# LayerNorm, attention and a SiLU feed-forward gate on one core: narrow attention matmuls joined, transposes and normalizations moved, the start reordered

## The chip, the cores and the metric

The kernel runs on one core of a Trainium2 chip. The metric is the time of the device for one execution, in microseconds, lower is better. A run gives one such time; the time of a kernel is the median of its runs. Besides, one execution was recorded by the hardware profiler: its span runs from the first to the last instruction.

The core has five engines that run their own queues of instructions in order and wait for each other by semaphores: TensorE (PE; its weight loads are shown as PEld), VectorE (DVE), ScalarE (ACT), GpSimd (POOL), and SyncE (SP), which here only issues DMAs. Matmul results go to PSUM, in 8 banks; everything else lives in SBUF.

## The reference

```python
xn = layernorm(x)                                    # x: (4, 512, 512), over the last axis
q, k, v = (einsum('bpd,hde->bphe', xn, W) + b for W, b in ((W_Q, b_Q), (W_K, b_K), (W_V, b_V)))
scores = einsum('bqhe,bkhe->bhqk', q, k) / sqrt(128) # 16 heads of 128
attn = softmax(where(causal, scores, -1e5), axis=-1)
z = einsum('bkhe,bhqk->bqhe', v, attn)
s = einsum('bqhe,hed->bqd', z, W_O) + b_O
g = (xn @ gate_w.T) * gate_s                         # gate_w, up_w: (1408, 512), entries -1, 0, 1
u = (xn @ up_w.T) * up_s
f = ((silu(g) * u) @ down_w.T) * down_s
out = x + s * silu(f)
```

## The kernel before

Everything is float32. To keep that precision[...], each operand of a matmul is held as two tensors, a high part (rounded by a copy on ACT to fp32r) and a low part (the rest, by a subtraction, on DVE or POOL). A product is three matmuls, high x high, high x low and low x high: `mm3` (line 90) and `mm3_all` (line 95, all high x high first). The class `Split` carries the pair.

The program runs in two stages, each written in a fixed order by hand (`tc.manual_schedule()`): the order of the calls is the order in every engine's queue. The first stage is LayerNorm and attention, up to line 635. The second is the feed-forward part with the final product (`ffn`, line 640), in a branch chosen by a flag computed in the first stage (whether the ternary weights are exact in fp32r; here they are, so `ffn(True)` runs).

Attention works on 64 "heads": 8 groups `g` of two heads (HG = 2), in each group four batches `b`, in each batch the two heads `i`; `heads` (line 526) is that list and `n` the index in it. The 512 rows of a batch are four tiles of 128. `xnT[b]` is the normalized input, transposed.

One pass of the loop at line 534, for head `n`, issues:
- `softmax` (line 280): scores of this head, query tile by query tile in the order 3, 2, then 1 and 0 packed, each only against the keys it may see (512, 384, 256 and 128 columns); DVE adds the mask and takes the row extreme (L306); ACT computes exp with the row sum (L320), DVE the reciprocal of the sum (L323), POOL scales the row (L324).
- `turn_p` (line 327): the probabilities are transposed, by 32x32 blocks on DVE (L338) and by two DMAs through DRAM (L343, L349); they come back in `raw`, for the next pass of the loop.
- `split_p` (line 354): high and low part of the probabilities of the head before, `pt`, in two halves of 128x640: ACT casts (L365), DVE subtracts (L366). In the first four passes and the last one it stands right behind `softmax`, in the others behind `turn_p`. The very last head uses `transpose_p` on PE instead.
- `project` (line 250), a generator: q, then k of the next head, each twelve matmuls of 512 columns into one PSUM bank; ACT adds the bias and writes the high part (L260), DVE the low part (L263). The first head alone is done in two halves (`parts` = 2), in one PSUM tile.
- `attend` (line 384) for the head before: z is 4 query tiles wide; key tile j = 0, 3, 1, 2 contributes to the query tiles from j on, so its matmuls have 512, 128, 384 and 256 columns, in three passes. ACT and DVE then write z with its bias, high and low (L399, L400).
- `fill`: the projection of v, a row tile at a time (`project_v`, line 242, twelve matmuls of 256 columns), in passes with i = 0, two tiles ahead of `turn_p` and two at the end; in passes with i = 1 `project_out` (line 413), the output projection of the group and batch before, accumulated in DRAM over the groups.
- `split_pending` (line 160): casts and subtractions of weights that have arrived. `prepare` (line 166) issues their loads: on SP at the start, on ACT's queue in the loop (line 525). The staging pool `rawp` has 4 buffers.

In the passes n = 0, 2, 4 (`ln_next`) the LayerNorm of the next batch is finished: `ln_normalize` (line 218) on DVE behind q's projection, then, at the end of the pass, `ln_transpose` (line 227): four PE transposes of 128x128 a tile, an ACT cast, and the low part on DVE (`ln_low`). The statistics (`ln_stats`, `ln_sd`) are taken in the passes 0, 1 and 3. The square root and the exp need different tables on ACT; `table` loads one ahead of its use.

PSUM: pool `ps_st` has 3 banks, tag "st" (scores, transposes of even tiles, the warm-up); pool `ps_mm` has 5, tag "mm" (v, q, k, z, output projection, transposes of odd tiles). A tile takes the bank that was given out longest ago, and waits until its last reader is done. `pp`, the pool of the probabilities, has one buffer.

The start, lines 469 to 523, is written out: loads, twenty warm-up transposes (`warm_up`), statistics and normalization of batch 0 tile by tile, weight splits in between, and the first q, k and v.

## Time and profile before

| what | value |
|---|---|
| median of 3 runs (lowest, highest) | 1222.03 us (1222.0, 1223.22) |
| the profiled execution | 1223.04 us, its span 1221.2 us |
| PE clock granted over the span | 0.998 |
| instructions in the span | 18879 |
| POOL scaling the probabilities (L324), 256 of them | 148.8 us |
| DVE low part of the probabilities (L366), 126 | 133.0 us |
| ACT exp (L320), 256 | 140.9 us |
| DVE block transposes (L338), 378 | 113.3 us |

Busy time of the engines by stretch of the span, with the number of instructions in brackets; the columns are start and end, length, busy time of PE, PEld, DVE, ACT and POOL, PE's clock, the mean share of the DMA engines, GB/s:

```profile
0.00:22.00 22.00, 15.78 (x100) 13.87 (x101) 12.31 (x25) 11.65 (x23) 11.17 (x20) 1.00 0.55 176
22.00:50.00 28.00, 27.30 (x165) 23.64 (x164) 25.18 (x75) 16.31 (x35) 4.13 (x8) 1.00 0.48 157
50.00:100.00 50.00, 48.33 (x281) 41.93 (x281) 43.60 (x126) 30.31 (x67) 9.98 (x14) 1.00 0.45 136
...
400.00:600.00 200.00, 200.00 (x1129) 177.08 (x1129) 152.35 (x385) 90.19 (x212) 51.16 (x64) 1.00 0.66 201
```

The stretch from 0 to 22 us is the start, 22 to 100 holds the first passes with the LayerNorm of batches 1 to 3, the third kind is the steady middle. The attention stage ends near 974 us; behind it comes the feed-forward part. Matmuls are pipelined: a record's duration is longer than the distance to the next one's start, and that distance is what a matmul costs PE.

### The profile page before, as it was taken

What the parts mean: (1) busy time and instruction counts of PE and PEld (TensorE: products, weight loads), DVE (VectorE), ACT (ScalarE), POOL (GpSimd) and SP (SyncE); (2) the same over time, 40 slices, a digit from 0 to 9 for tenths busy, and PEclk for the clock granted to TensorE, in tenths of its full rate; (3) what the DMA queues carried; (4) which work ended last, traced back from release to release, by engine and by line L of the source; (5) the groups of instructions that cost most, each with busy time, mean ns of one, the idle gap of its engine ahead of it and who ended that gap; (6) DMA issues with size and microseconds to landing.
All of it is one profiled execution on the core that took longest, in us unless ns stands there. A gap on an engine that the chain in (4) does not pass through costs nothing.

```text
span 1221.2 us, 18879 instructions
## 1 busy us (share of the span) xinstructions
PE 1204.9 (99%) x6510; PEld 1049.7 (86%) x6510; DVE 827.3 (68%) x2044; ACT 526.0 (43%) x1169; POOL 303.2 (25%) x433
## 2 busy tenths in 40 slices
PE   7999999999999999999999999999999999999997
PEld 7878888888888888888888888888888888888886
DVE  6897777777777777777777676767677533434343
ACT  5654544444445445444544454445444342323231
POOL 4212321232124213321422141214121341212010
PEclk9999999999999999999999999999999999999999
DMA  4454456666675667666755565565544893737341
GB/s 161 134 177 146 142 171 199 197 193 192 190 207 173 198 201 210 180 199 201 222 182 173 178 190 170 174 191 174 173 156 156 270 317 94 207 87 212 82 147 38
DMA packets 117912, 215.55 MB, mean 177 GB/s; under 512 B 13232, under 2 KB 45744, under 8 KB 117808
## 3 DMA queue, kind: packets, MB, share of 16 engines
q1 hardware_dynamic: 74016, 134.51, 34.8%
q10 hardware_dynamic: 29376, 53.26, 14.5%
q0 software_dynamic: 14416, 26.48, 8.1%
q8 instruction: 53, 0.87, 0.3%
q14 instruction: 51, 0.42, 0.1%
HBM read 135.17 MB, written 79.04 MB: 175 GB/s over the span
## 4 chain that ended last, share of the span: by engine, by line
PE 95%; DVE 3%; ACT 1%; DMA 0%; issue 0%; SPq 0%; DVEq 0%; ACTq 0%
PE psv L103 14%; PE psq L103 14%; PE psk L103 14%; PE z L395 10%; PE pd L676 7%; PE pg L676 7%; PE pu L676 7%; PE pso L91 5%; PE pso L93 5%; PE pso L92 5%; PE sc L91 3%; PE sc L93 3%; PE sc L92 3%; DVE xn L224 1%; PE sc L297 1%; DVE xl L235 1%
## 5 line engine op out<-in xcount | busy, mean ns | idle before, releaser
L324 POOL TENSOR_SCALAR p<-p,rtot 128x512 f32<-128x512 f32 (+3 forms) x256 | 148.8, 603 | 673.7 <-DVE rtot L323 673.7
L320 ACT ACTIVATE p<-p,nmax 128x512 f32<-128x512 f32 (+3 forms) x256 | 140.9, 552 | 148.6 <-DVE nmax L306 148.6
L366 DVE TENSOR_TENSOR ptl<-ptr,pth 128x640 fp32r<-128x640 f32 x126 | 133.0, 1093 | 1.4 <-ACT pth L365 1.4
L338 DVE STREAM_TRANSPOSE sq<-p 128x256 f32<-128x256 f32 x378 | 113.3, 362 | 0.0
L306 DVE CUSTOM_DVE_ANT_0 p<-sc,mask 128x512 f32<-128x512 f32 (+2 forms) x192 | 96.5, 552 | 1.4 <-PE sc L93 1.4
L260 ACT ACTIVATE k<-psk,consts 128x512 fp32r<-128x512 f32 (+1 forms) x65 | 44.3, 681 | 108.7 <-PE psk L103 108.7
L260 ACT ACTIVATE q<-psq,consts 128x512 fp32r<-128x512 f32 (+1 forms) x65 | 44.3, 682 | 97.0 <-PE psq L103 71.7
L365 ACT CAST pth<-ptr 128x640 fp32r<-128x640 f32 x126 | 85.0, 724 | 0.8 <-DMA ptr<-turn 0.5
L421 DVE TENSOR_TENSOR a<-pso,a 128x512 f32<-128x512 f32 x108 | 72.1, 686 | 17.7 <-PE pso L93 17.7
L263 DVE SCALAR_TENSOR_TENSOR k<-psk,consts,k 128x512 fp32r<-128x512 f32 (+1 forms) x65 | 48.0, 738 | 52.9 <-ACT k L260 52.9
L702 DVE SCALAR_TENSOR_TENSOR hd<-pu,consts,sg 128x512 f32<-128x512 f32 x44 | 33.0, 751 | 66.7 <-PE pu L676 62.2
L323 DVE RECIPROCAL rtot<-tot 128x1 f32<-128x1 f32 x256 | 41.6, 163 | 42.7 <-ACT p L320 36.3
L91 PE MATMUL sc<-k,q 128*128 128x512 f32 (+2 forms) x192 | 65.9, 343 | 2.8 <-DVE xl L235 1.6
L93 PE MATMUL sc<-k,q 128*128 128x512 f32 (+2 forms) x192 | 64.7, 337 | 0.0
L92 PE MATMUL sc<-k,q 128*128 128x512 f32 (+2 forms) x192 | 64.7, 337 | 0.0
L263 DVE SCALAR_TENSOR_TENSOR q<-psq,consts,q 128x512 fp32r<-128x512 f32 (+1 forms) x65 | 47.6, 732 | 9.4 <-ACT q L260 9.4
L320 ACT ACTIVATION_READ_ACCUMULATOR p<-p,nmax 128x1 f32 x256 | 47.7, 186 | 0.0
L91 PEld LDWEIGHTS sc<-k,q 128*128 128x128 f32 x192 | 36.2, 188 | 9.2 <-DVE xl L235 3.5
L732 ACT ACTIVATE o<-o 128x512 f32<-128x512 f32 (+1 forms) x17 | 10.3, 607 | 68.8 <-DVE o L731 68.8
L92 PEld LDWEIGHTS sc<-k,q 128*128 128x128 f32 x192 | 36.2, 188 | 3.6
L93 PEld LDWEIGHTS sc<-k,q 128*128 128x128 f32 x192 | 36.1, 188 | 2.6
L700 ACT ACTIVATE sg<-pg,consts 128x512 f32<-128x512 f32 x44 | 30.3, 688 | 17.0 <-PE pg L676 17.0
(734 smaller groups left out, 3342.2 us busy)
## 6 DMA issues: line engine op xcount, KB each, us to landing
turn<-sq SPq DMA_DIRECT2D x63, 640.0 KB, 3.8
ptr<-turn SPq DMA_DIRECT2D x252, 160.0 KB, 3.4
acc<-a SPq DMA_DIRECT2D x124, 256.0 KB, 3.7
a<-acc ACTq DMA_DIRECT2D x108, 256.0 KB, 2.9
xt<-in_x SPq DMA_DIRECT2D x16, 256.0 KB, 4.2
wor<-in_w_o ACTq DMA_DIRECT2D x16, 256.0 KB, 4.9
fa<-acc SPq DMA_DIRECT2D x16, 256.0 KB, 5.7
fx<-in_x SPq DMA_DIRECT2D x16, 256.0 KB, 6.0
```

The source lines that it names most:

```text
L91: nc.tensor.matmul(ps, a.hi, b.lo, start=first, stop=False)
L92: nc.tensor.matmul(ps, a.hi, b.hi, start=False, stop=False)
L93: nc.tensor.matmul(ps, a.lo, b.hi, start=False, stop=last)
L103: nc.tensor.matmul(ps, l, r, start=n == 0, stop=n == len(todo) - 1)
L263: nc.vector.scalar_tensor_tensor(q.lo[:, at_], ps[:, at_], bias[:, h : h + 1], q.hi32[:, at_], ALU.add, ALU.subtract,)
L306: nc.vector.tensor_tensor_reduce(out=of[t], in0=where[t], in1=add, scale=-SCALE, scalar=BIG, op0=ALU.add, op1=ALU.min, accum_out=nmax[t],)
L320: nc.scalar.activation(of[t], of[t], AF.Exp, bias=nmax[t], scale=-1.0, accum_out=tot)
L324: nc.gpsimd.tensor_scalar(of[t], of[t], rtot, 1.0, ALU.mult, ALU.mult)
L338: nc.vector.transpose(dst.rearrange("p a s i -> p s a i"), src.rearrange("p (s a i) -> p s a i", s=n, i=Q),)
L366: nc.vector.tensor_tensor(dst(pt.lo), src, dst(pt.hi32), ALU.subtract)
L395: nc.tensor.matmul(o, v, p_, start=k == 0, stop=k == len(todo) - 1)
L676: nc.tensor.matmul(ps, l, r, start=first and k == 0, stop=last and k == len(pairs) - 1)
```

## The change

- `attend` gets an argument `joined`, true for the heads with index 9 to 60. There the passes run over the key tiles 0, 1, 2 only. Key tile 3 is computed apart in a PSUM tile `z2` of two parts: one matmul multiplies its high weights by the high and the low probabilities at once (256 columns), one adds low x high to the first part (128 columns). The probabilities' high and low parts lie in one tensor for that (`p_split`). ACT writes the first three query tiles from `z`; `z2` is copied to SBUF by ACT, its two parts and z's last tile are added on DVE, and the last query tile leaves from there.
- `split_p` gets `shared`: in the passes 9 to 61 the first half's subtraction goes to POOL.
- In the passes n = 2 and 4 the four normalizations of the next batch stand behind the four reciprocals of the softmax, one each, on DVE. In pass 0 they stay.
- In the passes 0, 2, 4 the sixteen transposes go one by one behind the matmuls of the last two v tiles, and the low parts with them (`side`), instead of all behind them.
- At the start the statistics of tiles 2 and 3 are taken together, ahead of the low parts of tiles 0 and 1; the exp table is loaded right after their square root; the low part of wv goes to DVE; wq and wk of the second head are split after the first head's q and k. `project` takes a PSUM tile for each part.
- Behind the last output projection stand eight more transposes of the identity, into a tile that nobody reads.

```diff
+LINGER = 8
...
         for n, (l, r) in enumerate(todo):
             nc.tensor.matmul(ps, l, r, start=n == 0, stop=n == len(todo) - 1)
+            if side:
+                side.pop(0)()
...
-        def split_w(dst, raw):
+        def split_w(dst, raw, on=nc.gpsimd):
             nc.scalar.copy(dst.hi, raw)
-            nc.gpsimd.tensor_tensor(dst.lo, raw, dst.hi32, ALU.subtract)
+            on.tensor_tensor(dst.lo, raw, dst.hi32, ALU.subtract)
...
-        def warm_up():
+        def warm_up(n=WARM):
...
-            for k in range(WARM):
+            for k in range(n):
...
         def ln_transpose(b, t):
+            for step in ln_transposes(b, t):
+                step()
+
+        def ln_transposes(b, t):
+
             xn = xn_of.pop((b, t))
             pool, tag = ((ps_st, "st"), (ps_mm, "mm"))[t % 2]
-            tr = pool.tile([P, ND, P], F32, name="tr", tag=tag)
-            for c in range(ND):
-                nc.tensor.transpose(tr[:, c, :], xn[:, ts(c, P)], ident)
             to = xnT[b][:, :, ts(t, P)]
-            nc.scalar.copy(to.hi, tr)
-            lo_of[b, t] = lambda: nc.vector.tensor_tensor(to.lo, tr, to.hi32, ALU.subtract)
+            tr = []
+
+            def step(c):
+                if c == 0:
+                    tr.append(pool.tile([P, ND, P], F32, name="tr", tag=tag))
+                nc.tensor.transpose(tr[0][:, c, :], xn[:, ts(c, P)], ident)
+                if c == ND - 1:
+                    nc.scalar.copy(to.hi, tr[0])
+                    lo_of[b, t] = lambda: nc.vector.tensor_tensor(
+                        to.lo, tr[0], to.hi32, ALU.subtract
+                    )
+
+            return [lambda c=c: step(c) for c in range(ND)]
...
-            ps = ps_mm.tile([P, S], F32, name="ps" + name, tag="mm")
...
             for k in range(parts):
                 at_ = ts(k, S // parts)
-                mm3_all(ps[:, at_], [(w[:, c, :], xnT[b][:, c, at_]) for c in range(ND)])
+                ps = ps_mm.tile([P, S // parts], F32, name="ps" + name, tag="mm")
+                mm3_all(ps, [(w[:, c, :], xnT[b][:, c, at_]) for c in range(ND)])
...
-        def softmax(qT, kT):
+        def softmax(qT, kT, between):
...
                     nc.vector.reciprocal(rtot, tot)
+                    if between:
+                        between.pop(0)()
                     nc.gpsimd.tensor_scalar(of[t], of[t], rtot, 1.0, ALU.mult, ALU.mult)
...
-        def split_p(raw):
-            pt = weight(pp, [P, NS, P], "pt", "pt")
+        def p_split():
+            both = pp.tile([P, 2, NS, P], F32R, name="pt", tag="pt")
+            pt = Split(both[:, 0], both[:, 1])
+            pt.both = both
+            return pt
+
+        def split_p(raw, shared):
+            pt = p_split()
...
-                nc.vector.tensor_tensor(dst(pt.lo), src, dst(pt.hi32), ALU.subtract)
+                on = nc.gpsimd if shared and k == 0 else nc.vector
+                on.tensor_tensor(dst(pt.lo), src, dst(pt.hi32), ALU.subtract)
...
-        def attend(h, pt, vs):
+        def attend(h, pt, vs, joined):
             z = ps_mm.tile([P, NT, P], F32, name="z", tag="mm")
+            last = NT - 1
+            e = ts(h % HG, E)
+            s_ = slot[last]
...
-                for j in (0, NT - 1, 1, 2):
-                    v = getattr(vs[j], part)[:, ts(h % HG, E)]
+                for j in range(last) if joined else (0, last, *range(1, last)):
+                    v = getattr(vs[j], part)[:, e]
...
+            if joined:
+                z2 = ps_mm.tile([P, 2, P], F32, name="z2", tag="mm")
+                nc.tensor.matmul(z2, vs[last].hi[:, e], pt.both[:, :, s_, :], start=True, stop=False)
+                nc.tensor.matmul(
+                    z2[:, 0], vs[last].lo[:, e], pt.hi[:, s_, :], start=False, stop=True
+                )
...
-            nc.scalar.activation(zT.hi, z, AF.Identity, bias=bias)
-            nc.vector.scalar_tensor_tensor(zT.lo, z, bias, zT.hi32, ALU.add, ALU.subtract)
+            def leave(at_, src):
+                nc.scalar.activation(zT.hi[:, at_], src, AF.Identity, bias=bias)
+                nc.vector.scalar_tensor_tensor(
+                    zT.lo[:, at_], src, bias, zT.hi32[:, at_], ALU.add, ALU.subtract
+                )
+
+            if not joined:
+                leave(slice(0, NT), z)
+                return zT
+            leave(slice(0, last), z[:, :last])
+            rest = small.tile([P, 2, P], F32, name="rest", bufs=1)
+            nc.scalar.copy(rest, z2)
+            nc.vector.tensor_tensor(rest[:, 0], rest[:, 0], rest[:, 1], ALU.add)
+            nc.vector.tensor_tensor(rest[:, 1], z[:, last], rest[:, 0], ALU.add)
+            leave(last, rest[:, 1])
             return zT
...
-            ln_stats(0, [2])
             split_pending(-4)
             ln_transpose(0, 0)
             ln_transpose(0, 1)
+            split_pending(-3)
+            ln_stats(0, [2, 3])
             ln_low(0, 0)
             ln_low(0, 1)
-            ln_sd(0, [2])
-            split_pending(-3)
-            ln_stats(0, [3])
-            split_pending(-2)
-            ln_sd(0, [3])
+            ln_sd(0, [2, 3])
+            table(AF.Exp)
             ln_normalize(0, 2)
             ln_normalize(0, 3)
+            split_pending(-2, nc.vector)
...
-            split_pending(-1)
-            table(AF.Exp)
             qT = next(q_of)
             kT = next(k_of)
+            split_pending(-1)
...
+                joined = B * HG < heads.index(before) < len(heads) - 3
...
+                norms = [lambda t=t: ln_normalize(b + 1, t) for t in range(NT)] if ln_next else []
+                of = softmax(qT, kT, norms if n > 0 else [])
...
-                    pt = split_p(raw)
+                    pt = split_p(raw, B * HG < n < len(heads) - 2)
...
-                    if ln_next:
-                        for t in range(NT):
-                            ln_normalize(b + 1, t)
+                    while norms:
+                        norms.pop(0)()
...
                 if ln_next:
+                    for t in range(NT):
+                        side.extend(ln_transposes(b + 1, t))
+                        side.append(lambda t=t: ln_low(b + 1, t))
                     fill(range(half, NT))
-                    for t in range(NT):
-                        ln_transpose(b + 1, t)
-                        ln_low(b + 1, t)
+                    while side:
+                        side.pop(0)()
...
+            warm_up(LINGER)
```

More of the change, by code (lines that the diff above doesn't have):

```diff
@@ L103, in mm3_all @@
             nc.tensor.matmul(ps, l, r, start=n == 0, stop=n == len(todo) - 1)
+            if side:
+                side.pop(0)()
+    side = []
     with ExitStack() as at:
@@ L158, with split_pending @@
         pending = []
-        def split_pending(n):
+        def split_pending(n, on=nc.gpsimd):
             for due, dst, raw in [p for p in pending if p[0] <= n]:
-                split_w(dst, raw)
+                split_w(dst, raw, on)
             pending[:] = [p for p in pending if p[0] > n]
@@ L257, in project @@
                 at_ = ts(k, S // parts)
-                mm3_all(ps[:, at_], [(w[:, c, :], xnT[b][:, c, at_]) for c in range(ND)])
+                ps = ps_mm.tile([P, S // parts], F32, name="ps" + name, tag="mm")
+                mm3_all(ps, [(w[:, c, :], xnT[b][:, c, at_]) for c in range(ND)])
                 yield
-                nc.scalar.activation(
-                    q.hi[:, at_], ps[:, at_], AF.Identity, bias=bias[:, h : h + 1]
-                )
+                nc.scalar.activation(q.hi[:, at_], ps, AF.Identity, bias=bias[:, h : h + 1])
                 nc.vector.scalar_tensor_tensor(
-                    q.lo[:, at_], ps[:, at_], bias[:, h : h + 1], q.hi32[:, at_],
-                    ALU.add, ALU.subtract,
+                    q.lo[:, at_], ps, bias[:, h : h + 1], q.hi32[:, at_], ALU.add, ALU.subtract
                 )
@@ L365, in split_p @@
                 nc.scalar.copy(dst(pt.hi), src)
-                nc.vector.tensor_tensor(dst(pt.lo), src, dst(pt.hi32), ALU.subtract)
+                on = nc.gpsimd if shared and k == 0 else nc.vector
+                on.tensor_tensor(dst(pt.lo), src, dst(pt.hi32), ALU.subtract)
             return pt
         def transpose_p(of):
-            pt = weight(pp, [P, NS, P], "pt", "pt")
+            pt = p_split()
             pairs = [(j, t) for j in range(NT) for t in range(j, NT)]
@@ L531, in attend_last @@
                 g, b, i = before
-                zs.setdefault((g, b), []).append(attend(g * HG + i, pt, v_of[g, b]))
+                joined = B * HG < heads.index(before) < len(heads) - 3
+                zs.setdefault((g, b), []).append(attend(g * HG + i, pt, v_of[g, b], joined))
             for n, (g, b, i) in enumerate(heads):
@@ L556 @@
                 if n == 1:
-                    pt = split_p(raw)
-                of = softmax(qT, kT)
+                    pt = split_p(raw, B * HG < n < len(heads) - 2)
+                norms = [lambda t=t: ln_normalize(b + 1, t) for t in range(NT)] if ln_next else []
+                of = softmax(qT, kT, norms if n > 0 else [])
                 if n > 1 and early:
-                    pt = split_p(raw)
+                    pt = split_p(raw, B * HG < n < len(heads) - 2)
                 look()
@@ L566 @@
                 if not early:
-                    pt = split_p(raw)
+                    pt = split_p(raw, B * HG < n < len(heads) - 2)
                 split_pending(n)
@@ L632 @@
             last = (NG - 1, B - 1)
-            zs[last].append(attend(H - 1, pt, v_of[last]))
+            zs[last].append(attend(H - 1, pt, v_of[last], False))
             for t in range(NT):
                 project_out(*last, t, zs[last])
+            warm_up(LINGER)
     def ffn(exact):
```

## The prediction

> **What bounds the kernel now.** I read the shares of part 1 of the page first, then the chain of part 4, then PE's waits over the whole run, then the timeline of one head in the middle, and last the chain and the timelines of the first 66 us.
>
> ```profile
> PE 1204.9 (99%) x6510; PEld 1049.7 (86%) x6510; DVE 827.3 (68%) x2044; ACT 526.0 (43%) x1169; POOL 303.2 (25%) x433
> ...
> PE 95%; DVE 3%; ACT 1%; DMA 0%; issue 0%; SPq 0%; DVEq 0%; ACTq 0%
> ```
>
> TensorE is the bound: 99% busy, 95% of the chain. Work on DVE, ACT or POOL counts only where PE waits for it. PE's waits (who, for whom, us, times, longest) are few, and all but the last lie before 67 us:
>
> ```profile
> PE sc L91 <- DVE xl L235: 1.6, 4, 0.6
> PE tr L232 <- DVE xn L224: 1.5, 3, 0.8
> PE warm L216 <- POOL ident masks.py:199: 1.4, 1, 1.4
> PE psq L103 <- DVE q L263: 1.4, 1, 1.4
> ...
> PE pg L676 <- PE pso L93: 0.9, 1, 0.9
> ```
>
> From 100 to 900 us PE has no wait at all; there only its own instruction stream can be shortened. One attention product (`attend`) in PE's timeline, columns start, duration, line, tiles, shape:
>
> ```profile
> 506.12 0.39 PE L395 MATMUL z<-pth,v_0h 128*128 128x512 f32 x1
> ...
> 506.35 0.22 PE L395 MATMUL z<-pth,v_3h 128*128 128x128 f32 x1
> ...
> 506.41 0.39 PE L395 MATMUL z<-pth,v_1h 128*128 128x384 f32 x1
> ...
> 506.64 0.28 PE L395 MATMUL z<-pth,v_2h 128*128 128x256 f32 x1
> ...
> 506.75 0.40 PE L395 MATMUL z<-pth,v_0l 128*128 128x512 f32 x1
> ...
> 508.04 0.64 PE L103 MATMUL psv<-wv4h,xh 128*128 128x256 f32 x4
> ```
>
> The distance of starts is the cost, not the duration. A pass of four takes 0.64 us, the twelve 1.92 (506.12 to 508.04). The 384-wide one takes 0.23 here; in the scores, where no narrow one stands before it, 0.175 (511.61, 511.78, 511.96). So a 128-wide matmul costs its 0.06 and about 0.06 more at its successor: 0.12, as much as a 256-wide one (0.117).
>
> **What the Trainium skill says.** "TensorE: Matmul & The Clock Gate", section Back-to-back issue gap: the spacing is set by weight load and matmul together. The trace agrees (128 columns cost as much as 256), but not with the page's 81 and 131 ns for N=128 and 512: here 120 and 230, which I use. "SBUF — State Buffer", section SBUF: two separate sides: DVE and POOL share a port pair as an exclusive lock, taken by a DVE op in a two-port mode, or with two SBUF inputs against a POOL op that reads SBUF. The trace agrees:
>
> ```profile
> 10.31 1.66 DVE L224 TENSOR_SCALAR xn<-xt,mv,rstd 128x512 f32<-128x512 f32 x1
> 10.39 2.70 POOL L145 TENSOR_TENSOR wv0l<-wvr,wv0h 128x512 fp32r<-128x512 f32 x2
> ```
>
> The same `xn` takes 0.55 where POOL is idle. "GPSIMD Engine Reference", section Engine selection: two-input elementwise work is about twice as slow on POOL; the trace has 1.29 us for a 128x512 subtraction on POOL and 0.69 on DVE.
>
> **Joined narrow matmuls (52 heads).** `joined` holds for head indices 9 to 60. Three 128-wide matmuls (key tile 3) leave the passes; one 256-wide (high values on high and low weights side by side) and one 128-wide come behind them, in another PSUM tile. Cost: 3 x (0.23 + 0.175 + 0.117) + 0.117 + 0.12 = 1.80. L297 and L298 of the scores are the same pair of shapes: 512.48, 512.60, 512.66, then 0.29 for a 512-wide one instead of 0.23, so the pair's price is measured. Gain 1.92 - 1.80 = 0.12 a head, 52 x 0.12 = **6.2 us**. Bounds: 0.13 a head (6.8) at best, 0 if new waits eat it.
>
> What it adds elsewhere, per head. ACT: one 0.69 becomes 384 wide (0.60 by the exp of that width), a copy of 256 (0.37, the v cast) and 128 wide (0.39): +0.67. DVE: 0.75 becomes about 0.60 + 2 x 0.285 + 0.29: +0.7; the shared `split_p` takes a 128x640 subtraction (0.77 to 0.81) off it: even. POOL gets that half: 1.29 x 640/512 = 1.6 us, 53 times. The work that hides all this is PE's 14.8 us per head. The new waits: ACT's last `leave` waits for two DVE adds; behind it stand the v casts (or the next exp, which waits for DVE anyway). After z ends at 508.0 the chain of four ACT and DVE steps is over by about 510.5; `pso` reads z first at 512.6. POOL's half starts when its normalizing ends (516.6) and ends near 518.2; the third pass reads it at 522.2. In the heads that also split weights, POOL's subtractions now block DVE's `ptl` (two take 3.56 at 532.92 instead of 1.52) and leave 0.5 us before the third pass; with one half gone from DVE this gets better. ACT's loads of raw weights wait for POOL in seven heads (q copied at 241.65 after 4.27 us of it, k's low part 0.77 before the scores); POOL idles 1.71 us just before, and the half fits there but for some 0.3. The PSUM ring of five now turns over eight tiles a head: `psv` of tile 3 takes the bank of the same head's `psq`, free at 505.5 (at 537.1 in the worst kind of head), needed at 509.3 (539.0). I take 0 for all of this.
>
> **The start (before 21.1).** Own PSUM tiles per half in `project` remove the 1.4 us wait of the second `psq` for the first half's DVE read. The low half of wv goes from POOL to DVE, so nothing locks `xn` of tiles 2 and 3 (1.66 and 1.30 become 0.55), and PE's 0.3 and 0.75 before their transposes go. Against this: the statistics of tile 3 (0.69 + 0.18) now stand on DVE ahead of both `xl`; the third pass of the first `psq` starts at 10.3 instead of 9.46. The Exp table (1.28 + 0.2) now sits on ACT ahead of the wv casts, which then end at 11.95, before `psv` wants them at 13.3; SP's queue is unchanged. Step by step: psk ends 12.4, transposes to 13.3, psv to 14.75, second psq at 14.75 instead of 16.87, less 0.1 for psk waiting on the first psq's bank. **Gain 2.0**, bounds 1.2 and 2.6.
>
> **Transposes between matmuls, and the norms (heads 0, 2, 4).** The chain in head 0 runs on DVE from 26.95 to 37.2: statistics, q, norms, k, v, xl. In head 0 the norms stay behind q's projection, so xn of tile 0 ends at 32.13, but its first transpose is now PE's second instruction of the fill, at 30.0: PE stops 2.1 us there. Then 39 instructions at 0.117 reach 36.7, and the scores run unhindered to 38.4. Before, tile 3's scores began at 34.80 and waited for xl; they ended at 37.90. **Cost 0.5.** In head 2 the norms go between the softmax reciprocals, where DVE idles 1.6 us in all. Each pair takes 0.65, and by the lock POOL's normalizing and DVE's norm exclude each other. Unlocked, `ptl` ends at 57.5, 0.45 after the third pass wants it, and the scores end at 64.8 instead of 66.64 (gain 1.8). Locked throughout it ends at 58.9, PE stops 1.9, and they end at 66.3 (gain 0.3). I take **0.7**, since rtot frees POOL about when the norm starts. In head 4 only 0.24 was lost (3.83 for transposes and scores against 3.59 of work): **0.2**.
>
> **LINGER.** Eight transposes behind the last `pso`: the first `pg` (974.62) waits for DVE's last `a_last` (973.72 + 0.69), so PE is idle from 973.5 and eight at 0.115 fill 0.9 of it. **Cost 0.1** for the last one's completion; bounds 0 and 0.9.
>
> **Sum.** 6.2 + 2.0 - 0.5 + 0.7 + 0.2 - 0.1 = 8.5 us. The profiled execution took 1223.04 (span 1221.2, 1.8 around it), which gives 1214.5; it lies 1.0 above the median of 1222.03, and against that I predict **1213.5**.
>
> **Rivals.**
> A. The head of the run gives nothing: ACT's table load and DVE's added work delay `psv`, and head 2 pays the lock in full. For: all steps there hang on 0.1 to 0.5 us. Against: the 1.4 of PSUM wait goes whatever else happens; 1.4 less the 0.8 of the later third pass leaves 0.6 of the 2.0, and head 2 turns from 0.7 to -0.4. 8.5 - 1.4 - 1.1 = 6.0: 1216.0.
> B. The middle is taken back by a new wait, for instance `psv` of tile 3 behind `psq`'s read where ACT waits for POOL. For: 0.77 us is the smallest distance found. Against: it exists in 7 heads of 52. Then only 2.3 remain: 1219.7.
> C. Slower. In-order ACT, blocked at the last `leave`, passes its delay on to the casts that free PSUM, and PE stops in every joined head. Place: psv of tile 3 and the first scores after it. It decides from 8.5/52 = 0.17 us of stop per head, which needs DVE's two adds some 2 us later than worked out (k's low part ends 2.7 to 3.05 before the scores in most heads). At 0.25 a head: 13 - 8.5 = 4.5: 1226.5. Against: DVE's load per head is unchanged.
> D. That joining changes nothing, because the pair costs three narrow ones: excluded by L297 and L298, save for the wider stride; counted in B.
>
> **How the numbers follow.** Forecast 0.73 (own range 1211.5 to 1216), A 0.12, B 0.10, C 0.05. The range 1210.5 to 1218.5 takes in A and the bounds of the terms (the start 0.6 better, head 2 1.1 better, a wait or two in the middle). 0.2%, 2.4 us, is what a measurement of this kernel can tell from no change; faster than 1219.6 are the forecast, A and half of B: 0.90; same 0.05, slower 0.05.
>
> **What will show it.** z's group with z2 at 1.80 from first start to the next matmul; no PE wait from 100 to 900; first scores near 19.1; a wait of about 2 us of the first transpose for xn in head 0; `ptl` against the third pass in head 2; `pg` within 0.2 of `a_last`. A PE wait for DVE or POOL that recurs in the joined heads would make the prediction wrong.

## The result: four microseconds faster, less than half of the forecast

| | before | changed |
|---|---|---|
| median of 8 runs each (lowest, highest) | 1222.39 us (1221.67, 1224.16) | 1218.81 us (1217.08, 1219.66) |
| ratio, 95% interval | | 0.9967 (0.9956 to 0.9977) |
| the profiled execution: time, span | 1223.04, 1221.2 us | 1218.36, 1217.0 us |

The kernel is 0.33% faster, 3.6 us by the medians. The forecast was 8.5 us and a range from 1210.5 to 1218.5; the median lies just outside it. The page after the change, parts 1 and 4 (busy us, share of the span, instructions; then the chain's shares):

```profile
PE 1199.1 (99%) x6466; PEld 1047.4 (86%) x6466; DVE 795.5 (65%) x2149; ACT 549.9 (45%) x1272; POOL 378.6 (31%) x484
...
PE 96%; DVE 2%; ACT 0%; DMA 0%; issue 0%; SPq 0%; DVEq 0%; ACTq 0%
```

TensorE is still the bound, with 44 matmuls fewer (52 saved, 8 idle ones added). All its waits, in the order of the forecast's list (who, for whom, us, times, longest):

```profile
PE z L423 <- DVE pt L391: 3.4, 1, 3.4
PE tr L247 <- DVE xn L230: 2.2, 2, 2.0
PE warm L222 <- POOL ident masks.py:199: 1.4, 1, 1.4
PE psq L104 <- DVE xl L250: 1.3, 1, 1.3
PE sc L92 <- DVE k L280: 1.1, 1, 1.1
PE psq L104 <- ACT xh L249: 0.7, 1, 0.7
```

All lie before 100 us. The first line is new and the largest: z's third pass in head 2 waits 3.4 us for the low part of the probabilities. The waits alone do not tell the price, though. ("z group" is the run of z matmuls of one `attend`.) To get the price, the first matmul of each of the 64 z groups, which the timeline gives to 0.01 us, was set against the same group of the kernel before. That difference is a running account; where it changes, something was won or lost:

| stretch, profiled executions | forecast, us | measured, us |
|---|---|---|
| start, to the first scores (21.09 to 19.03) | +2.0 | +2.06 |
| head 0, to the first z group | -0.5 | -0.58 |
| head 1, to the second z group | 0 | +0.23 |
| head 2, to the third (19.08 before, 21.86 after) | +0.7 | -2.78 |
| head 4, to the fifth | +0.2 | +0.35 |
| 52 joined heads (the account goes from -0.72 to +5.20) | +6.2 | +5.92 |
| LINGER, to the first `pg` | -0.1 | -0.08 |
| after the first `pg`, to the end of the span | 0 | -0.96 |
| sum | +8.5 | +4.16 |

The spans differ by 4.2, so the account is closed. Against the forecast's 8.5, 3.5 us are lost in head 2, 1.0 at the very end and 0.3 in the joined heads; some 0.4 more than forecast came in at the start and in heads 1 and 4, which leaves 4.3 missing. The start of one profile is good to 1 us only: in the ten other profiles below that have the changed start the first scores come at 18.03 to 18.92, here at 19.03. The joined heads read as forecast:

```profile
505.38 0.40 PE L423 MATMUL z<-pt,v_0h 128*128 128x512 f32 x1
...
505.91 0.28 PE L426 MATMUL z<-pt,v_3h 128*128 128x256 f32 x1
506.03 0.22 PE L427 MATMUL z<-pt,v_3l 128*128 128x128 f32 x1
506.09 0.69 PE L104 MATMUL psv<-wv4h,xh 128*128 128x256 f32 x4
```

The group, which begins at 504.33, ends with the wide and the narrow matmul behind the three passes: 1.76 us to the next instruction (506.09). The four `psv` matmuls behind it start 0.52 before the next four instead of 0.47, because a narrow one stands before them; with this 0.05 the group costs 1.81, the forecast's 1.80.

**Head 2.** The timelines of DVE, POOL and PE in the changed kernel:

```profile
51.59 0.97 DVE L230 TENSOR_SCALAR xn<-xt,mv,rstd 128x512 f32<-128x512 f32 x1
...
54.68 0.65 DVE L230 TENSOR_SCALAR xn<-xt,mv,rstd 128x512 f32<-128x512 f32 x1
55.26 3.69 DVE L391 TENSOR_TENSOR pt<-ptr,pt 128x640 fp32r<-128x640 f32 x2
```

```profile
51.59 0.70 POOL L342 TENSOR_SCALAR p<-p,rtot 128x512 f32<-128x512 f32 x1 [9.89 <-DVE rstd L228]
...
55.16 3.10 POOL L151 TENSOR_TENSOR wo0l<-wor,wo0h 128x512 fp32r<-128x512 f32 x2
```

```profile
55.35 0.28 PE L423 MATMUL z<-pt,v_2l 128*128 128x256 f32 x1
58.99 0.50 PE L423 MATMUL z<-pt,v_0h 128*128 128x512 f32 x1 [3.37 <-DVE pt L391]
...
60.09 0.27 PE L247 MATMUL tr<-ident,xn 128*128 128x128 f32 x1
60.11 0.38 PE L104 MATMUL psv<-wv0h,xh 128*128 128x256 f32 x1
60.31 0.39 PE L247 MATMUL tr<-ident,xn 128*128 128x128 f32 x1
...
62.21 0.41 PE L247 MATMUL tr<-ident,xn 128*128 128x128 f32 x1
62.28 0.56 PE L104 MATMUL psv<-wv0l,xh 128*128 128x256 f32 x1
62.64 0.41 PE L247 MATMUL tr<-ident,xn 128*128 128x128 f32 x1
```

Two things went wrong one after the other. The four norms now stand ahead of `pt` on DVE. Each runs beside a scaling on POOL and takes 0.97, 0.87, 0.76 and 0.65 us instead of 0.55, which is the lock that the forecast reckoned with. So `pt`'s two subtractions run at 55.26, just where POOL subtracts the two parts of wo0 (55.16); they take 3.69 us instead of the 1.64 of the kernel before, where POOL came to wo0 only when they were done:

```profile
54.91 1.64 DVE L366 TENSOR_TENSOR ptl<-ptr,pth 128x640 fp32r<-128x640 f32 x2 [0.46 <-ACT pth L365]
```

```profile
56.64 2.56 POOL L145 TENSOR_TENSOR wo0l<-wor,wo0h 128x512 fp32r<-128x512 f32 x2 [1.50 <-ACT wo0h L144]
```

Then, 1.3 us after PE has resumed, every pair of a transpose and a matmul takes 0.43 us (62.21 to 62.64) instead of 0.22 (60.09 to 60.31). The table by stretches shows why (us, busy time and instructions of PE, PEld, DVE, ACT and POOL, PE's granted clock, DMA):

```profile
56.90:60.30 3.40, 1.30 (x9) 1.26 (x10) 3.40 (x7) 0.37 (x1) 1.36 (x1) 1.00 0.00 0
60.40:63.70 3.30, 3.30 (x17) 3.30 (x16) 3.30 (x8) 1.40 (x3) 0.00 (x0) 0.50 0.47 195
63.80:67.20 3.40, 3.40 (x27) 3.27 (x26) 2.72 (x7) 1.92 (x4) 0.00 (x0) 1.00 0.36 97
```

The clock was halved, from 60.33 for 3.413 us by its record: 1.7 us of work lost. In the kernel before it is at full speed from 5.18 to 1216.92, in this place too:

```profile
60.30:63.70 3.40, 2.74 (x22) 2.25 (x21) 3.30 (x8) 2.13 (x5) 0.00 (x0) 1.00 0.49 174
```

### The profile page after: what moved, and what is told of

Same layout as the page of the kernel before. It is cut to its first block, busy times and chain, and to the rows that moved or that the text cites. A ratio compares the mean times of both kernels' runs of the same rounds, so it can differ in the third digit from the quotient of the medians.

```text
span 1217.0 us, 19221 instructions
## 1 busy us (share of the span) xinstructions
PE 1199.1 (99%) x6466; PEld 1047.4 (86%) x6466; DVE 795.5 (65%) x2149; ACT 549.9 (45%) x1272; POOL 378.6 (31%) x484
## 4 chain that ended last, share of the span: by engine, by line
PE 96%; DVE 2%; ACT 0%; DMA 0%; issue 0%; SPq 0%; DVEq 0%; ACTq 0%
PE psv L104 15%; PE psq L104 14%; PE psk L104 14%; PE z L423 9%; PE pd L727 7%; PE pg L727 7%; PE pu L727 7%; PE pso L92 5%; PE pso L93 5%; PE pso L94 5%; PE sc L92 3%; PE sc L93 3%; PE sc L94 3%; PE sc L313 1%; PE tr L247 1%; PE z L426 1%
## 5 line engine op out<-in xcount | busy, mean ns | idle before, releaser
L391 POOL TENSOR_TENSOR pt<-ptr,pt 128x640 fp32r<-128x640 f32 x53 | 83.7, 1580 | 8.8 <-ACT pt L389 8.4
L389 ACT CAST pt<-ptr 128x640 fp32r<-128x640 f32 x126 | 85.0, 724 | 0.1
L469 DVE TENSOR_TENSOR a<-pso,a 128x512 f32<-128x512 f32 x108 | 69.4, 682 | 0.3 <-issue 0.3
L391 DVE TENSOR_TENSOR pt<-ptr,pt 128x640 fp32r<-128x640 f32 x73 | 68.8, 953 | 1.1 <-ACT pt L389 1.1
L423 PE MATMUL z<-pt,v_0h 128*128 128x512 f32 x128 | 50.7, 396 | 3.4 <-DVE pt L391 3.4
L423 PE MATMUL z<-pt,v_1h 128*128 128x384 f32 x128 | 44.2, 345 | 0.0
L92 PEld LDWEIGHTS sc<-k,q 128*128 128x128 f32 x192 | 36.2, 188 | 5.3 <-DVE k L280 1.3
```

The lines of the kernel that those rows point to most:

```text
L92: nc.tensor.matmul(ps, a.hi, b.lo, start=first, stop=False)
L391: on.tensor_tensor(dst(pt.lo), src, dst(pt.hi32), ALU.subtract)
L423: nc.tensor.matmul(o, v, p_, start=k == 0, stop=k == len(todo) - 1)
```

## Experiments

Each kernel is the changed one (or, where said, the one before) with one edit. "Second to third z" is the distance that head 2 sets; "falls" are the stretches of halved clock in the profiled execution, those at its very start and end left out. The experiments ran in three sets, each with runs of the kernel before beside them, to which the ratios refer. The ratios of E2 and E9 lie below that of the changed kernel (0.9967) with intervals that hardly touch its own, E6's and E8's lie above; the other times cannot be told from the changed kernel's, and there the stretches of the profile decide.

| | median, us | ratio to before (95%) | second to third z | falls at |
|---|---|---|---|---|
| E1 norms back | 1219.1 | 0.9971 (0.9959, 0.9983) | 20.84 | 30.6, 61.3 |
| E2 wo0 later | 1215.24 | 0.9943 (0.9929, 0.9957) | 18.16 | none |
| E3 stop filled | 1219.0 | 0.9964 (0.9950, 0.9977) | 20.29 | 30.2 |
| E4 plain transposes, head 2 | 1218.39 | 0.9967 (0.9955, 0.9979) | 22.09 | 30.1, 60.9 |
| E5 joined alone, on before | 1218.66 | 0.9966 (0.9954, 0.9979) | 19.10 | none |
| E6 start alone, on before | 1220.78 | 0.9986 (0.9980, 0.9993) | 19.09 | none |
| E7 plain transposes, head 0 | 1217.13 | 0.9961 (0.9947, 0.9975) | 22.78 | 57.1 (two long) |
| E8 norms on POOL | 1223.71 | 1.0011 (1.0002, 1.0019) | 20.51 | 34.2 (two long) |
| E9 three edits | 1215.68 | 0.9943 (0.9930, 0.9957) | 17.96 | none |
| E10 joined from head 5 | 1217.26 | 0.9955 (0.9941, 0.9969) | 17.93 | none |
| E11 no share for POOL | 1219.14 | 0.9965 (0.9952, 0.9979) | 21.85 | 30.1, 60.8 |

**E1, the norms back behind q's projection.**

```diff
-                of = softmax(qT, kT, norms if n > 0 else [])
+                of = softmax(qT, kT, [])
```

> The changed kernel with one part undone: the norms of heads 2 and 4 stand behind q's projection again; everything else as in the changed kernel. Measure: the distance from head 0's... second z group (first matmul) to the third one, 19.08 us in the kernel before, 21.86 in the changed one. Theory (the norms ahead of pt push pt's low part into POOL's wo0 split, the DVE/POOL lock stretches it from 1.64 to 3.69 us, the third pass stops 3.37 us, and this stop halves the granted clock for 3.41 us, at 1.7): no stop of the third pass, clock 1.00 throughout 54 to 70 us, instead the first transpose waits about 1.5 us for xn; distance about 18.8, so some 3.1 us faster than the changed kernel, near 1215.7 (6.7 below before). Rival (the clock falls because transposes stand singly between matmuls, or after any stop of 1 to 2 us): the clock is halved for about 3.4 us here too, distance about 20.5, near 1217.4.

The third pass no longer stops, but the first transpose now waits 2.4 us, not 1.5, and the clock falls all the same, at 61.3:

```profile
PE tr L247 <- DVE xn L230: 4.4, 2, 2.4
```

```profile
57.90:61.30 3.40, 1.34 (x12) 1.35 (x13) 3.27 (x12) 0.90 (x3) 0.96 (x1) 1.00 0.47 193
61.30:64.70 3.40, 3.40 (x19) 3.40 (x18) 3.38 (x6) 1.47 (x4) 0.00 (x0) 0.50 0.57 146
```

20.84 is the rival's number; the time, 1219.1, is above both expected ones (1215.7 and 1217.4). So a stop need not be 3.4 us long: 2.4 is enough, and in head 0 of this run the stop of 2.0 us for `xn`, which the changed kernel has too, was followed by a fall at 30.6. Putting the norms back does not help, since the transposes at their new place want them earlier than DVE has them.

**E2, the wo0 split of head 2 behind z's matmuls.**

```diff
-                split_pending(n)
+                if n != 2:
+                    split_pending(n)
...
                     attend_last(before, pt)
+                if n == 2:
+                    split_pending(n)
```

> The changed kernel with the split of wo0 in head 2 (two ACT casts, two POOL subtractions) moved behind z's matmuls; the norms stay between the reciprocals. Theory (lock): pt's two subtractions start at 55.3 as before but take about 1.65 together instead of 3.69; the third pass stops about 1.3 instead of 3.37 us; too short for the clock, which stays at 1.00; distance from the second to the third z group 21.86 - 2.05 - 1.7 = 18.1; near 1215.1. Rival 1 (it is the length of the work queued ahead on DVE, not the lock): the stop stays above 2.8 us and the time within 1 us of the changed kernel. Rival 2 (the clock falls for another reason than the stop's length): stop 1.3 but the clock halved all the same: distance 19.8, near 1216.8.

As the theory has it: 18.16, and 1215.24 for its 1215.1. The subtractions of `pt`, with the norms still ahead of them, take 1.54, the stop is 1.2 us, the clock stays up. (The waits for `xn` are those of the start and of head 0, 0.45 and 2.01.)

```profile
54.39 1.54 DVE L391 TENSOR_TENSOR pt<-ptr,pt 128x640 fp32r<-128x640 f32 x2
```

```profile
PE tr L247 <- DVE xn L230: 2.5, 2, 2.0
PE sc L92 <- DVE k L280: 2.0, 2, 1.1
...
PE z L423 <- DVE pt L391: 1.2, 1, 1.2
```

18.16 against 19.08 before is a gain of 0.9 in head 2, near the forecast's 0.7. But all of it is given back in the next head: the third to the fourth z group takes 16.04 instead of 14.81, since PE, earlier now, waits 0.94 us for k's low part, where DVE has four tiles of statistics ahead of it. From the second to the fourth z group E2 takes 34.20, the kernel before 33.89. So even without the collision the moved norms and transposes of head 2 bring nothing by themselves. This version has the lowest median of all kernels here, 3.6 below the changed one; one of its five executions, the slowest (1217.25), has a granted clock of 0.997 like one with a fall.

```profile
77.17 0.50 PE L92 MATMUL sc<-k,q 128*128 128x512 f32 x1 [0.94 <-DVE k L280]
```

**E3, the stop filled, and E4, the transposes of head 2 plain.** E3 puts 24 transposes of the identity, which nothing reads, between the second and third pass; E4 takes the steps out of `side` before `fill`. First E3's edit, then E4's:

```diff
             for k, (o, v, p_) in enumerate(todo):
+                if h == 1 and len(zs) == 1 and k == 8:
+                    warm_up(24)
                 nc.tensor.matmul(o, v, p_, start=k == 0, stop=k == len(todo) - 1)
```

```diff
+                    steps = side[:]
+                    if n == 2:
+                        side.clear()
                     fill(range(half, NT))
-                    while side:
-                        side.pop(0)()
+                    for step in side or (steps if n == 2 else []):
+                        step()
+                    side.clear()
```

> The changed kernel with 24 transposes of the identity (not used by anything; 24 x 0.117 = 2.8 us) put on PE between the second and the third pass of the z group that stops in head 2. They fill the stop and don't shorten it: the third pass still begins when pt's low part is there (59.0). Theory (PE idle for 3.4 us lowers the granted clock): clock 1.00 from 54 to 70 us, distance from the second to the third z group 21.86 - 1.7 = 20.15, near 1217.1. Rival (the clock falls because of the interleaved transposes that follow): the clock is halved from about 60.3 on as in the changed kernel, distance 21.9, no time gained.

> The changed kernel with the 16 transposes of head 2 behind the 24 psv matmuls, as in the kernel before, instead of singly between them; the norms stay between the reciprocals. Theory (the stop of 3.37 us lowers the clock, interleaving costs nothing): same stop, clock halved for about 3.4 us from about 60.3 on, distance 21.9 (+0.3 at most for a late xl). Rival (the interleaving lowers the clock): same stop, clock 1.00, distance 20.2, near 1217.1.

In head 2 both are as the theory has them. E3: 20.29, and with idle work in the stop the clock stays at 1.00. But its median is 1.9 above the theory's 1217.1 and no better than the changed kernel's: its profile has the fall in head 0, which that of the changed kernel lacks, takes 0.5 longer from the third to the fourth z group and 0.8 longer in one head near 357 us. E4: with no interleaving in head 2 the clock is halved all the same, 22.09. First the stretch after the stop in E3, then that in E4:

```profile
60.90:64.30 3.40, 3.40 (x32) 3.40 (x31) 3.40 (x10) 2.41 (x5) 0.00 (x0) 1.00 0.33 136
```

```profile
60.90:64.20 3.30, 3.30 (x18) 3.30 (x16) 3.30 (x9) 0.83 (x2) 0.00 (x0) 0.50 0.40 166
```

So it is PE's idleness, not the order of what it runs after the stop, that lowers the clock.

**How much idleness.** The clock's changes in every trace lie on a grid of 3.413 us that begins at another point in each execution: its stretches at one speed last 3.413, 6.827, 23.893, 27.307 us and so on, whole multiples. The share of each grid stretch in which PE had no matmul running, worked out from the matmul records (whose ends are modelled, and of which a few can be missing):

| stop | idle in the worst grid stretch | clock after it |
|---|---|---|
| start, kernel before | 40% | full |
| head 0, changed kernel (26.20 to 29.61) | 44% | full |
| head 0, E2 | 50% | full |
| head 0, E1, E3, E4, E11 | 59% | halved |
| head 2, changed kernel and E1 | 61% | halved |
| head 2, E4, E7, E11 | 67, 70, 82% | halved |
| head 0, E8 | 68% | halved |

The limit lies between 50% and 59%. The same stop of 2.0 us in head 0 was followed by a fall in four profiled executions and by none in two, and where the grid cut it is what differed. A stop of 3.4 us leaves at least 1.7 in one stretch; in all four profiles that have it and don't fill it the clock fell. In E7 and E8 the stretch after the fall was itself 26% and 59% idle, and the halved clock lasted for two stretches; after each of the other falls the next stretch was not idle at all, and it lasted for one. The Trainium skill, "TensorE: Matmul & The Clock Gate", section Part 1: The HAM clock gate, has the free-running 3413 ns window and the half clock, and the traces agree; it puts the fall after a whole idle window, and there the traces differ: a stretch in which PE worked 41% of the time was followed by a fall.

The granted clock is known for every run. Profiles with two single falls show 0.996, those with one 0.997, those with none 0.998 (0.999 in E5). Of the eight runs of the changed kernel five have 0.996 (median 1219.22 us) and three 0.997 (1217.37): most of its executions probably pay for head 0 too, which its profile does not show. This is a sign and no proof: the figure also takes in the halved clock at the end of the span (2.6 to 6.2 us in these profiles), and executions of one kernel differ by 2 us or more without a fall (E9: 1214.8 to 1217.4, all at 0.998 or 0.999).

**E5 and E6, the kernel before with the joined matmuls alone, and with the changed start alone.** E5 has the diff's parts in `p_split`, `split_p`, `transpose_p`, `attend` and `attend_last`, E6 those in `split_w`, `split_pending`, `project` and the written-out start, and nothing else.

> The kernel before with the joined narrow matmuls alone (and POOL's share of the probabilities' low part, which came with them). Theory (52 heads at 0.114 us, nothing given back): z's group 1.76 instead of 1.91 us in the joined heads, from the tenth z group to the sixty-first 748.8 us instead of 754.6, no PE wait from 100 to 900 us; 5.9 us faster than before, near 1216.7, ratio 0.9952. Rival (new waits in the heads that split weights eat part of it, or the end of attention comes late): PE waits in the middle, less than 3 us, near 1220.

> The kernel before with the changed start alone (own PSUM tile for each half of the first q and k, joint statistics of tiles 2 and 3, low half of the first wv on DVE, Exp table earlier). Theory: first scores at 18.2 to 19.0 us instead of 21.1, and all of it is kept to the first z group (43.45 before, about 41 here); 2 to 2.9 us faster, near 1220.2, ratio 0.998. Rival (the DVE chain of head 0, not PE, sets when tile 3's scores start, so that the gain is lost there): first z group within 0.5 of 43.45, time within 0.5 us of before.

E5: no PE wait from 90 to 960 us, the tenth to the sixty-first z group takes 748.84, the first `pg` comes 5.86 us earlier. Its time is only 4.2 below before (1222.84 in the runs beside it), not the theory's 5.9, because the stretch from the first `pg` to the end is 1.6 longer. E6: first scores at 18.81, first z group 2.30 earlier, first `pg` 2.24, time 2.1 below: all kept. Together the two parts bring the first `pg` forward by 8.1 us, the whole change by 5.1. Norms, interleaving and LINGER cost 3.0 in these profiles.

**E7, the transposes of head 0 plain** (E4's edit, for n = 0).

> The changed kernel with the 16 transposes of head 0 behind the psv matmuls, as before, instead of singly between them. Theory (the interleaving puts a stop of 2.0 us at the first transpose, worth 0.5 to 0.6 by itself, and where more than half of one of the clock's 3.41 us stretches is idle, 1.7 more): no PE stop over 1.0 us between 20 and 50 us, no fall of the clock there, from first scores to first z group 22.3 us instead of 22.94; near 1217.4 as a median (0.6 and about half of 1.7 below the changed kernel). Head 2 is untouched: its stop of 3.4 us and the fall of the clock at about 60 stay. Rival (the earlier transposes pay in head 0, since xh and xl come earlier): first scores to first z group 23.2 or more, no gain.

First scores to first z group 22.36, no stop over 1 us there, no fall, median 1217.13: the theory's numbers. The first to the second z group takes 12.33 as in the kernel before, not the 12.11 of the changed one, as it does in E9 and E10 (E8 has 12.11), so the early transposes of head 0 seem to have won the 0.2 of head 1. Head 2 kept its stop, and the grid cut it so that the clock fell for two stretches. Two of its five executions have 0.998 and 0.999, as without any fall, and they are not its fastest (1219.22 and 1217.13).

**E8, the norms on POOL** (with E7's edit for head 0).

```diff
-            nc.vector.tensor_scalar(xn, xt, mv[:, 0:1], rstd, ALU.subtract, ALU.mult)
+            on.tensor_scalar(xn, xt, mv[:, 0:1], rstd, ALU.subtract, ALU.mult)
...
-                norms = [lambda t=t: ln_normalize(b + 1, t) for t in range(NT)] if ln_next else []
-                of = softmax(qT, kT, norms if n > 0 else [])
+                norms = [lambda t=t: ln_normalize(b + 1, t, nc.gpsimd) for t in range(NT)] if ln_next else []
+                of = softmax(qT, kT, [])
+                while norms and n > 0:
+                    norms.pop(0)()
```

> The changed kernel with the norms of heads 0, 2 and 4 computed by POOL (0.70 us each by its 128x512 scaling) instead of DVE, in heads 2 and 4 behind the four scalings of the probabilities, and with head 0's transposes plain as in the run before this one. DVE keeps only the reciprocals of 0.15. Theory (DVE's order of work sets the stops of the first five heads, and the clock falls only with such a stop): pt's low part is ready at or within 0.5 us of the third pass in head 2, clock 1.00 from 6 us to the end, second to third z group 17.3 to 17.8 us; head 3 may keep a stop of about 1 us for k; some 2 us better than the run with the wo split moved, near 1213. Rival (POOL's norms and DVE's subtraction of pt exclude each other as its wo split did): pt takes more than 3 us, the third pass stops 1.5 us or more, second to third z group 18.8 or more, near 1215 or above.

A miss for the theory. The rival has the distance (20.51) and the time right, but not the mechanism: `pt` takes 1.62, and z's third pass does not stop. From all instructions on the tile xn (duration in ns, min, median, max), and POOL's and DVE's timelines in head 2:

```profile
L230 POOL TENSOR_SCALAR xn<-xt,mv,rstd x12: 2057/2070/3285, 29.5 to 96.4; 128x512 f32<-128x512 f32 x12
```

```profile
58.70 9.46 POOL L230 TENSOR_SCALAR xn<-xt,mv,rstd 128x512 f32<-128x512 f32 x4
```

```profile
58.50 1.62 DVE L391 TENSOR_TENSOR pt<-ptr,pt 128x640 fp32r<-128x640 f32 x2 [0.21 <-ACT pt L389]
```

A norm takes POOL 2.07 us, not the 0.70 of its scaling: the transposes wait eight times, 7.6 us in all. The two differ in their second operand (one value per row, against a constant) and in one operation (subtract and multiply, against two multiplications); which of these costs the time was not tried. The lock goes the other way than the rival said: DVE's subtraction kept its 1.62 and POOL's first norm was stretched to 3.29. Here DVE started first, at 58.50 against 58.70. In the changed kernel POOL's first subtraction of wo0 started first (55.16 against 55.26) and kept its 1.30 us, while DVE's two took 1.88 each and POOL's second 1.84. So it may be the order of the starts that decides who is held up, and not the kind of the instruction; the two were not separated.

**E9, E10 and E11.** E9 takes E2's and E7's edits and moves two of head 3's four statistics ahead of `pt`; E10 is E9 joined from head 5; E11 is the changed kernel without the share. The parts of the edits that are new:

```diff
+                if n == 3:
+                    ln_stats(ln_b, range(NT), (0, 1))
                 if n > 1 and early:
...
-                        ln_stats(ln_b, range(NT))
+                        ln_stats(ln_b, range(NT), (2, 3) if n == 3 else None)
```

```diff
-                joined = B * HG < heads.index(before) < len(heads) - 3
+                joined = HG * HG < heads.index(before) < len(heads) - 3
```

```diff
-                    pt = split_p(raw, B * HG < n < len(heads) - 2)
+                    pt = split_p(raw, False)
```

> The changed kernel with the wo0 split behind z's matmuls in head 2, head 0's transposes plain, and in head 3 the statistics of two of the four tiles moved into DVE's gap of 1.9 us ahead of pt. Theory (each stop has its own cause in DVE's order, and the causes add up): no stop over 1.3 us after the first scores, clock 1.00 to the end in every execution, second to third z group 18.2, third to fourth 14.8 to 15.0 instead of 16.04 (head 3's stop for k goes), first scores to first z group 22.4; 1.8 us below the run with the wo0 split moved alone, near 1213.4. Rival (taking a stop away only moves it to the next instruction that DVE's chain feeds): third to fourth z group stays above 15.7, or the second to third rises above 18.8; no better than 1215.

> The run before this one, with the joined matmuls and POOL's share from head index 5 instead of 9 on (56 heads). Theory: four more heads at 0.114: 0.46 us less, seen as 0.46 between the fifth and the tenth z group; near 1213.0, too little for the times to tell. Rival (DVE has no room for the two adds in the early heads): a PE wait between 105 and 180 us and no gain.

> The changed kernel without POOL's share: DVE does both halves of the low part of the probabilities in every head, as in the kernel before. Theory (PE has cover for all of DVE's work in the middle, so POOL's share is worth nothing by itself): no PE wait from 100 to 900 us, tenth to sixty-first z group 748.8 us as with the share, time within 0.5 us of the changed kernel. Rival (with joining, DVE's adds use up what was left, 0.5 us in the heads that split weights): PE waits for pt in seven or so heads, 1 to 3 us in all, tenth to sixty-first z group 750 or more.

E9: second to third z 17.96, no falls, first `pg` at 965.79, the second earliest of all. But third to fourth is 15.91, as the rival said: the moved statistics waited 1.4 us for their rows of x, so only a part of the stop went. In time E9 cannot be told from E2. From the first scores to the fifth z group E9 takes 85.22 us, E2 85.90, the kernel before 85.49 and the changed one 88.27: with the collision and the falls gone, the moved norms and transposes gain 0.3 us at best, where the forecast had 0.4. E10: the fifth to the tenth z group is 0.46 shorter than in E9, as expected; its time is no better. E11: one stop in the middle, where POOL splits three weights and DVE's `pt` takes 3.00:

```profile
257.80 0.50 PE L423 MATMUL z<-pt,v_0h 128*128 128x512 f32 x1 [0.39 <-DVE pt L391]
```

It takes 0.96 us more over the 51 heads (749.79 for 748.83), between the two expectations. But with the share, too, E1, E2, E3 and E9 take 749.15 to 749.66, each 0.3 to 0.8 more in one head near 355 us, where PE waits in E3 (its only wait there from 100 to 960 us):

```profile
PE psv L104 <- DVE q L280: 0.6, 1, 0.6
```

So what POOL's share buys in the middle is between 0.1 and 1.0 us, and E11 has most of the latter back at the end, where it is 0.7 shorter. Its time, 1219.14, cannot be told from the changed kernel's, as the theory said.

**The end.** From the start of the last matmul to the end of the span it takes 6.93 us before and 6.94 in E6, but 7.19 in E11, 7.56 to 7.93 in the changed kernel, E2, E3, E4, E7 and E9, and 8.33 to 8.53 in E1, E5, E8 and E10. The work on DVE and ACT after that matmul is the same in all, and so is the issue of the last store, 2.13 or 2.14 us after it. What grows is SP's closing part, and it goes with the number of SP's records: 831 twice, then 836, 850 or 851, and 854. The extra records are semaphore instructions (327 in the changed kernel against 308). That the kernels with more of them on SP end later is what these thirteen profiles have in common; it was not tried by an experiment, and the cause stays open. For the changed kernel the metric shows only about half of it: its time is 1.3 to 1.4 us longer than its span in every execution, that of the kernel before 1.7 to 1.9, so the profiled executions differ by 4.7 us where the spans differ by 4.2.

## Why the prediction was wrong

**Where it failed.** The step that failed is the gain in head 2, put at 0.7 us where 2.8 were lost. "Locked throughout it ends at 58.9, PE stops 1.9" and "I take **0.7**" looked at one lock only, that between the norms and POOL's scaling of the probabilities. It asked what the moved norms do to `pt`, but not what stands on POOL when the delayed `pt` runs. The wo0 split was there. The forecast had written of the heads that split weights that "POOL's subtractions now block DVE's `ptl` (two take 3.56 at 532.92 instead of 1.52)", and did not count head 2 among them, because before the change the two missed each other: `ptl` was done at 56.5, POOL began at 56.64. The collision is worth some 2.1 us (E2: 1.54 instead of 3.69), and the forecast's worst case in that step, a gain of 0.3, was no bound. The lock that it did think of is real and lay between its two cases: PE's stop in E2 is 1.2 us, for 0.45 without the lock and 1.9 with it throughout. It also took head 2 alone, and did not ask what an earlier PE meets in head 3 (E2).

**What was not thought of.** The fall of the clock, 1.7 us in head 2 and, in many executions, 1.7 more in head 0. The forecast put the stop of 2.1 us in head 0 at the 0.5 that it delays the scores, and asked nothing about the clock. The page of the Trainium skill that it cites for the distance of matmuls, "TensorE: Matmul & The Clock Gate", describes this clock in its Part 1. Rival A came nearest in kind (head 2 pays), but with 1.1 lost there, where 3.5 were, and the start, which it took as lost in part, gave its 2.06. Rival B's number, 1219.7, lies nearest to the measured one, but by luck: the middle gave nearly all of its 6.2.

**The end.** The sum has no term for the end of the program, so it stands at nothing there without a reason; it took 1.0 us more in the profiles. Why is open; the profiles show only that SP has more semaphore instructions.

**What held.** The joined heads: 0.114 a head instead of 0.12, no PE wait in the middle, so rivals B and C did not come; a wait of B's kind, 0.6 us in one head, stands in E3 alone with the same middle. Of the covers taken at nothing, none cost PE a wait in the middle of the changed kernel. The start (2.06 against 2.0), head 0 without the fall (-0.58 against -0.5), head 4 and LINGER. The sign was forecast at 0.90; it was right with little room.

## What to carry to other kernels

Where an instruction is delayed, look not only at who waits for it but at what the other engines do at its new time, here DVE against POOL, and what the gain meets in the next stretch. Price a stop of PE by the grid of its clock, not by its length alone: here a stop that left more than about half of a 3.4 us stretch idle cost 1.7 us extra, and idle transposes in the stop kept the clock up. Set a kernel's repeated groups against those of the one before, one by one; the running difference tells which part paid and which took.

## What the hardware showed that was not expected

- PE's clock was halved after a grid stretch that was only 59 to 61% idle, stayed up at 50%, and stayed halved after one that was 26% idle (E7).
- POOL's TENSOR_SCALAR over 128x512 took 2.07 us as subtract and multiply with two per-row operands, and 0.70 as two multiplications with one and a constant; DVE's took 0.55 with two.
- When DVE's and POOL's subtractions collided, both sides lost: DVE's two took 3.69 instead of 1.64, POOL's two 3.10 instead of 2.56. When DVE's subtraction started 0.2 us ahead of POOL's norm, DVE lost nothing and the norm took 3.29 instead of 2.07.
- The closing part of the program took 4.8 to 6.4 us after the last store was issued, longer where SP had more semaphore instructions; why is open.
